# Sorted rows of the first halves loaded in blocks of 32 features and turned by VectorE

## Chip, cores and metric

The kernel runs on one core of a Trainium2 chip. The metric is the device time of one execution in microseconds; lower is better. The time before is the median of three runs.

## What is computed

The input x is (4, 32, 128, 128) in float32: four batches. Layer 0 splits each image into 128 channels of 64 x 64 positions and lets the channels' *columns* attend to each other within a batch. Layer 1 takes each batch as 8,192 rows of 128 features (written `t` below), adds linear attention, and then a mixture of experts:

```python
def _L1_ffn_ref(x, router_w, router_b, expert_w, expert_b):
    router_probs = jax.nn.softmax(x @ router_w + router_b, axis=-1)   # 8 experts
    top_p, top_i = jax.lax.top_k(router_probs, 2)
    top_p = top_p / jnp.sum(top_p, axis=-1, keepdims=True)
    expert_out = jnp.einsum('bnd,edc->bnec', x, expert_w) + expert_b
    gathered = jnp.take_along_axis(expert_out, top_i[..., None], axis=2)
    return jnp.einsum('bnk,bnkc->bnc', top_p, gathered)
...
t = t + _L1_attn_ref(_ln_t(t), L1_attn_Wk, L1_attn_Wq, L1_attn_Wv)
t = t + _L1_ffn_ref(_ln_t(t), L1_ffn_router_w, L1_ffn_router_b, L1_ffn_expert_w, L1_ffn_expert_b)
```

The change is in the experts: each row is multiplied by the 128 x 128 weights of its two experts only. The kernel handles a batch as 32 tiles of 128 rows, in two halves of 16 tiles.

## The kernel before

**The main loop: layer 0's attention, in ticks.** `attend` walks over blocks of 512 x 512 scores. One step of its inner loop is a *tick*: TensorE multiplies a 128 x 512 block of scores (L609, `pe<-qn,qn`), ScalarE takes its exponential (L612, `pr<-pe`), and two ticks later TensorE multiplies the result with the values (L497, `po<-pr,qT`). As scores are symmetric, each block is used a second time, turned: VectorE turns its 32 x 32 blocks (L421, `F<-pr`), `move` writes F to DRAM after four ticks (L530, `blocks<-F`, one DMA), and `bring`, three ticks later, reads it back with the groups of 32 swapped (L545, `F<-blocks`, six DMAs). The products with it (`transposed_share`, L433, `pg<-F,qT`) are put on a list (`late`) with a due time: LAG = 57 clock units after `bring`. A tick counts 8 units, and 4 more when it takes such a share, so with all three matmuls it counts 12. VectorE adds the result to the output (L442, `o<-o,pg`).

**The order.** Instructions of TensorE, VectorE, ScalarE and SP are kept in the order in which the program writes them. Other work is interleaved as generators: while batch b+1 runs through `attend`, the closing of batch b (`layer1`) is advanced by two yields a tick, one in front of the tick's matmuls and one behind them, at most once in PACE = 10 units. So one yield of `layer1` is half a tick.

**Layer 1 of a batch.** `close_rows` finishes layer 0's rows and normalises them; `attention_rows` adds the attention. Its input tiles are turned without TensorE already: `fetch_blocks` (L938, `blocks<-rows`) reads rows from DRAM in four DMAs, each bringing 32 features of all rows to 32 partitions, in pieces of 128 B, and VectorE turns the 32 x 32 blocks (L950). Then `route` chooses two experts for each row, and `sorted_experts(h)` runs for each half h. Batch 3 has no batch behind it to hide in: it multiplies all experts (`last_parts`) and doesn't sort. So `sorted_experts` runs for three first halves and three second halves.

**`sorted_experts(h)`.** It gives each (row, expert) pair of a half a place in a list sorted by expert, in which each expert's part begins at a new tile: NT = 2 x 16 + 8 - 1 = 39 tiles of 128 places. GpSimd scatters the rows with their weight to `xs[h]` in DRAM (L1066, rows of DW = 132 elements: 128 features, then the weight four times, 528 B). When all are there, the tiles are read, multiplied by the weights of the tile's expert, and written to `ys`; GpSimd then gathers two rows of `ys` for each token and adds them.

The read-and-multiply part is what changes. It takes the 39 tiles in 20 *pairs*. For each pair it

- loads both tiles with one DMA from SP (`load`, L1096, `xn<-xs`, 132 KB) into one of six buffers, which lie in the tile `xn` that the scattered rows came from,
- turns them on TensorE three steps later (L1137, `pys<-ident,xn`, 128 x 128 each) into a PSUM bank,
- copies the turned pair to SBUF with ScalarE (L1106, `xn<-pys`),
- multiplies each tile by its expert's weights (L1130, `pys<-ew_sb,xn`), at a column that TensorE reads from a register, in the step after,
- multiplies the result by the row's weight, which came in column D of the loaded tile, with VectorE (L1112, `results<-pys,xn`), and stores it (L1116, `ys<-results`, 128 KB).

A step is two yields, so one tick: the load, and the evictions of the step before, are at the first yield, the matmuls at the second. There are 25 steps, so 50 yields.

`hold` gives out the PSUM banks for such side work. At most three are held; when a fourth is asked for, the oldest is evicted at once. `wait_for` adds a wait: loads wait until all scatters of the half have landed, and the next batch's scatters wait for the loads.

Of the kernel before, what the change touches and what calls it, by code (L numbers as in the profile page):

```python
# [12 lines left out]
F32 = mybir.dt.float32  # L13
# [3 lines left out]
ALU = mybir.AluOpType  # L17
# [5 lines left out]
def kernel(  # L23
# [43 lines left out]
    nc = tc.nc  # L67
    P = 128
# [8 lines left out]
    S = 32  # L77
    NH, KQ, D = wk.shape
    E = router_w.shape[1]
# [10 lines left out]
    stat = ctx.enter_context(tc.tile_pool(name="stat", bufs=2))  # L90
# [27 lines left out]
    NT = 2 * HR + E - 1  # L118
    DW = D + 4
# [5 lines left out]
    ew_sb = const.tile([P, E, D], F32, tag="ew", name="ew_sb")  # L125
    xs = [dram.tile([NT * P, DW], F32, tag=f"xs{h}", name=f"xs_{h}", bufs=1) for h in range(2)]
    xs_made, xs_read = ([], []), ([], [])

    def wait_for(inst, others, why):
        for other in others:  # L130
            tc.add_manual_dep(
                inst, other.name, mybir.DependencyInfo(mybir.DependencyClass.Sync, mybir.DependencyReason.DATA),
                reason=why,
            )
# [56 lines left out]
    def hold(name, evict, alloc=psum_t):  # L191


        while len(held) >= banks[0]:
            held[0]()
        bank = alloc(name)

        def done():
            if done in held:
                held.remove(done)  # L200
                evict(bank)

        held.append(done)
        return bank, done
# [449 lines left out]
    def layer1(b, st):  # L654
# [3 lines left out]
        xn = big1.tile([P, KT, DW], F32, tag="xn", name=f"xn_{b}")  # L658
# [6 lines left out]
        begin = stat.tile([P, 2, NT + 1], U32, tag="begin", name=f"begin_{b}", bufs=1)  # L665
# [3 lines left out]
        keep = {}  # L669
# [273 lines left out]
        def attention_rows(u):  # L943
# [35 lines left out]
            if u % 2:  # L979
                for _ in route(u // 2):  # L980
                    yield
                    yield
                yield
                yield
                yield from sorted_experts(u // 2)

        def sorted_experts(h):
# [5 lines left out]
            half = slice(r0, r0 + HR)  # L993
# [21 lines left out]
            pc, done = hold(f"pcnt_{b}_{h}", lambda p: nc.vector.tensor_copy(counts.rearrange("p n e -> p (n e)"), p[:, : 2 * E]))  # L1015
# [5 lines left out]
            count = counts[:, 1, :][:, :, None]  # L1021
# [30 lines left out]
            ys = dram.tile([NT * P, D], F32, tag=f"ys{h}", name=f"ys_{b}_{h}")  # L1052

            def offset(ap):
                return bass.IndirectOffsetOnAxis(ap=ap, axis=0)
# [4 lines left out]
            for n in range(2 * HR):  # L1060
                i, k = n // HR, r0 + n % HR
                if n % HR == 0:
# [3 lines left out]
                inst = nc.gpsimd.indirect_dma_start(  # L1066
                    xs[h], offset(place[:, i, k : k + 1]), xn[:, k, :], None
                )
# [20 lines left out]
            bufs = [xn[:, r0 + 2 * i : r0 + 2 * i + 2, :] for i in range(8)]  # L1089
            pairs = [(g, min(2, NT - 2 * g)) for g in range((NT + 1) // 2)]  # L1090

            def rows_of(dram_rows, g, n):
                return dram_rows[2 * g * P : (2 * g + n) * P, :].rearrange("(j p) d -> p j d", p=P)

            def load(g, n):
                inst = nc.sync.dma_start(bufs[g % 6][:, :n], rows_of(xs[h], g, n))  # L1096
                wait_for(inst.ins, xs_made[h], "a tile holds tokens of any row")
                xs_read[h].append(inst.ins)

            def products(turned, applied):  # L1100


                def leave(p):
                    if turned:
                        g, n = turned
                        nc.scalar.activation(  # L1106
                            bufs[6 + g % 2][:, :n, :D], p[:, : n * P].rearrange("p (j t) -> p j t", t=P), AF.Copy
                        )
                    if applied:
                        g, n = applied  # L1110
                        result = keep["results"][:, g % 4]
                        nc.vector.tensor_tensor(  # L1112
                            result[:, :n], p[:, 2 * P : 2 * P + n * D].rearrange("p (j c) -> p j c", c=D),
                            bufs[g % 6][:, :n, D : D + 1].to_broadcast([P, n, D]), ALU.mult,
                        )
                        nc.sync.dma_start(rows_of(ys, g, n), result[:, :n])  # L1116

                p, done = hold(f"pys_{b}_{h}_{(turned or applied)[0]}", leave)
                if applied:
                    g, n = applied  # L1120
                    if g % 2 == 0:
                        _, at = nc.values_load_multi_w_load_instructions(
                            begin[0:1, h, 2 * g : min(2 * g + 4, NT)], engines=[mybir.EngineType.PE], min_val=0,
                            max_val=(E - 1) * D,
                            skip_runtime_bounds_check_because="D times a count of at most E - 1, never negative",
                        )
                        begins[:] = at
                    weights = ew_sb.rearrange("p e c -> p (e c)")
                    for j in range(n):
                        nc.tensor.matmul(  # L1130
                            p[:, 2 * P + j * D : 2 * P + j * D + D], bufs[6 + g % 2][:, j, :D],
                            weights[:, bass.ds(begins[2 * (g % 2) + j], D)], start=True, stop=True,
                        )
                if turned:
                    g, n = turned
                    for j in range(n):
                        nc.tensor.transpose(p[:, ts(j, P)], bufs[g % 6][:, j, :D], ident)  # L1137
                return done

            if "results" not in keep:  # L1140
                keep["results"] = work.tile([P, 4, 2, D], F32, tag="df", name=f"results_{b}", bufs=1)
            done = None
            begins = []
            for at in range(len(pairs) + 5):
                if at < len(pairs):
                    load(*pairs[at])
                if done:
                    done()
                yield
                turned, applied = (pairs[at - d] if 0 <= at - d < len(pairs) else None for d in (3, 4))  # L1150
                done = products(turned, applied) if turned or applied else None
                yield
            if done:
                done()
            if h == 1:
                st["sorted"] = True
            yield from idle(1)
# [271 lines left out]
    for b in range(B):  # L1429
# [12 lines left out]
        done = [0] * len(timed)  # L1442
        start = clock[0]
        closing = None
        for half, _ in enumerate(chain(attend(b, states[b]), finish() if b == B - 1 else ())):
            if half % 2 == 0:
                t = 100 * (clock[0] - start) / UNITS
# [64 lines left out]
```

## Time and profile before

| | us |
|---|---|
| median of 3 runs | 1651.85 (1651.45 to 1653.72) |
| the profiled execution | 1650.83 |
| its span, first to last instruction | 1649.0 |

The profile is of one execution. PE is TensorE's matmuls, PEld its weight loads, DVE is VectorE, ACT ScalarE, POOL GpSimd, SP the engine that issues most DMAs; "SPq" is its queue of instructions. Durations of matmuls overlap, since TensorE is pipelined, so the time that a matmul takes from the next is read in the chain of work that ended last rather than from its duration. A group's line gives the engine, the operation, what is written and read, the shape, the count, then busy us and mean ns, then idle time just before and what ended it. A line of waits gives total us, times, and the longest. A line of a stage window gives its length, then busy us and counts of PE, PEld, DVE, ACT and POOL, the granted clock, the mean busy share of the 16 DMA engines (it can exceed 1, as packets overlap) and GB/s.

The whole span by 40 slices of 41 us, the busy share in tenths: TensorE is at 8 or 9 in every slice but the last.

### The profile page before, as it was taken

How to read it: one execution, taken by the hardware profiler on the slowest of the kernel's cores; microseconds unless marked ns; L12 is line 12 of the kernel's file. 1: busy time of each engine (PE TensorE's matmuls, PEld its weight loads, DVE VectorE, ACT ScalarE, POOL GpSimd, SP SyncE). 2: the span in 40 equal slices, each digit the busy share in tenths (PEclk: the TensorE clock that was granted, in tenths of full speed). 3: DMA queues.
4: the chain of work that ended last, by engine and by line, in shares of the span. 5: the costliest groups of instructions: out<-in, count | busy, mean ns of one | idle time of the engine just before them, and what ended most of it. 6: DMA issues, size and time to landing. Idle time of an engine off the chain costs nothing.

```text
span 1649.0 us, 21309 instructions
## 1 busy us (share of the span) xinstructions
PE 1609.9 (98%) x5192; PEld 846.5 (51%) x5192; DVE 931.5 (56%) x2383; ACT 898.5 (54%) x2839; POOL 593.8 (36%) x565
## 2 busy tenths in 40 slices
PE   8999999999999999999999999999999999999987
PEld 4444544455554455555554455555554455555633
DVE  4543353567586443549478443448658634345786
ACT  3555445466475555547556455556656555545386
POOL 1000000001015441446555543256555652437166
PEclk9999999999999999999999999999999999999999
DMA  4655656676759777997899777798699877886001
GB/s 143 205 179 178 197 187 213 222 231 204 168 196 283 239 222 220 266 257 200 211 221 287 253 236 241 222 268 230 196 209 279 275 248 236 248 251 192 14 14 39
DMA packets 304297, 345.37 MB, mean 209 GB/s; under 512 B 82096, under 2 KB 230704, under 8 KB 289840
## 3 DMA queue, kind: packets, MB, share of 16 engines
q1 hardware_dynamic: 269712, 304.50, 59.9%
q0 software_dynamic: 26624, 25.58, 7.6%
q10 hardware_dynamic: 7840, 13.93, 2.9%
q8 instruction: 44, 0.72, 0.2%
q14 instruction: 77, 0.63, 0.1%
HBM read 167.08 MB, written 182.09 MB: 212 GB/s over the span
## 4 chain that ended last, share of the span: by engine, by line
PE 81%; DVE 7%; DMA 5%; ACT 3%; SPq 2%; issue 1%; POOL 1%; ACTq 0%; DVEq 0%; POOLq 0%
PE po L497 24%; PE pe L609 23%; PE pg L433 20%; PE pys L1130 3%; PE py L1304 3%; PE pg L453 2%; PE pys L1137 2%; PE pgram L725 2%; DMA F<-blocks 1%; DVE F L421 1%; DMA blocks<-rows 1%; SPq L938 1%; ACT pr L612 1%; ACT xn L696 1%; DMA blocks<-F 1%
## 5 line engine op out<-in xcount | busy, mean ns | idle before, releaser
L612 ACT ACTIVATE pr<-pe 128x512 f32<-128x512 f32 (+1 forms) x576 | 322.4, 560 | 547.5 <-PE pe L609 507.0
L497 PE MATMUL po<-pr,qT 128*128 128x512 f32 (+3 forms) x1152 | 549.4, 559 | 4.2 <-ACT o L502 3.9
L609 PE MATMUL pe<-qn,qn 128*128 128x512 f32 x896 | 458.8, 594 | 4.6 <-ACT pr L612 4.6
L433 PE MATMUL pg<-F,qT 128*128 128x512 f32 x880 | 449.8, 593 | 4.7 <-DMA F<-blocks 4.7
L421 DVE STREAM_TRANSPOSE F<-pr 128x512 f32<-128x512 f32 x440 | 305.4, 700 | 134.5 <-ACT pr L612 124.7
L497 PEld LDWEIGHTS po<-pr,qT 128*128 128x128 f32 x1152 | 215.2, 190 | 250.2 <-issue 217.9
L1178 POOL DMA_INDIRECT acc<-ys,place x128 | 202.1, 1579 | 209.1 <-ACT pr L612 134.8
L438 ACT ACTIVATE junk<-F 128x512 bf16<-128x512 f32 x440 | 273.0, 620 | 4.9 <-DMA F<-blocks 4.9
L433 PEld LDWEIGHTS pg<-F,qT 128*128 128x128 f32 x880 | 166.8, 190 | 199.4 <-issue 182.3
L1066 POOL DMA_INDIRECT xs<-xn,place x192 | 186.0, 969 | 184.1 <-ACT pr L612 118.9
L609 PEld LDWEIGHTS pe<-qn,qn 128*128 128x128 f32 x896 | 155.6, 191 | 119.1 <-issue 106.7
L442 DVE TENSOR_TENSOR o<-o,pg 128x512 f32<-128x512 f32 x110 | 75.1, 683 | 205.4 <-PE pg L433 205.2
L1112 DVE TENSOR_TENSOR results<-pys,xn 128x256 f32<-128x256 f32 x120 | 49.9, 416 | 187.2 <-ACT xn L1106 168.5
L164 POOL TENSOR_TENSOR rn<-ss,neg_half 128x8 f32<-128x8 f32 (+1 forms) x17 | 27.2, 1602 | 320.0 <-DVE ss L296 319.9
L612 ACT ACTIVATION_READ_ACCUMULATOR pr<-pe 128x1 f32 x576 | 111.9, 194 | 0.0
L1106 ACT ACTIVATE xn<-pys 128x256 f32<-128x256 f32 x120 | 45.2, 377 | 111.4 <-PE pys L1137 111.4
L1130 PEld LDWEIGHTS pys<-ew_sb,xn 128*128 128x128 f32 x468 | 70.5, 191 | 52.2 <-issue 49.7
L609 PE MATMUL pe<-qn 128*128 128x512 f32 (+3 forms) x256 | 91.4, 440 | 0.7 <-ACT qn L342 0.7
L1178 POOL DMA_INDIRECT yb<-ys,place x64 | 60.8, 950 | 81.1 <-DMA F<-blocks 31.1
L438 ACT ACTIVATION_READ_ACCUMULATOR junk<-F 128x1 f32 x440 | 84.5, 192 | 0.0
L1130 PE MATMUL pys<-ew_sb,xn 128*128 x468 | 71.6, 275 | 0.0
L1304 PE MATMUL py<-ew_sb,xn 128*128 128x512 f32 x128 | 61.5, 622 | 5.1 <-ACT tmp L1260 3.9
(217 smaller groups left out, 1463.2 us busy)
## 6 DMA issues: line engine op xcount, KB each, us to landing
blocks<-F SPq DMA_DIRECT2D x110, 1024.0 KB
F<-blocks SPq DMA_DIRECT2D x220, 192.0 KB
F<-blocks SPq DMA_DIRECT2D x220, 128.0 KB
xn<-xs SPq DMA_DIRECT2D x114, 132.0 KB
ys<-results SPq DMA_DIRECT2D x114, 128.0 KB
F<-blocks SPq DMA_DIRECT2D x220, 64.0 KB
below<-F SPq DMA_DIRECT2D x31, 384.0 KB
T<-in_x_dram SPq DMA_DIRECT2D x64, 128.0 KB
```

The costliest lines, as they stand in the source:

```text
L421: f()
L433: nc.tensor.matmul(pg.rearrange("p (a f) -> p a f", a=4), st["qT"][i][:, ib, :], G[:, :, ib], start=(ib == 0), stop=(ib == NJ - 1),)
L438: nc.scalar.activation(junk, G[:, :, ib], AF.Copy, accum_out=st["sums"][:, NJ * i + ib, jc : jc + 1])
L442: nc.vector.tensor_tensor(st["o"][jc], st["o"][jc], pg, ALU.add)
L497: nc.tensor.matmul(row["po"][:, lo:hi], qT[blk // NJ][:, blk % NJ, :], w, start=start, stop=(row["left"] == 0))
L609: nc.tensor.matmul(pe[:, c0:], qn[jc][:, ts(j, P)], qn[i][:, c0:], start=True, stop=True)
L612: nc.scalar.activation(pr[:, c0:], pe[:, c0:], AF.Exp, accum_out=sums[:, t, i : i + 1]).ins
L1066: inst = nc.gpsimd.indirect_dma_start(xs[h], offset(place[:, i, k : k + 1]), xn[:, k, :], None)
L1112: nc.vector.tensor_tensor(result[:, :n], p[:, 2 * P : 2 * P + n * D].rearrange("p (j c) -> p j c", c=D), bufs[g % 6][:, :n, D : D + 1].to_ ...
L1130: nc.tensor.matmul(p[:, 2 * P + j * D : 2 * P + j * D + D], bufs[6 + g % 2][:, j, :D], weights[:, bass.ds(begins[2 * (g % 2) + j], D)], st ...
L1178: inst = nc.gpsimd.indirect_dma_start(to, None, ys, offset(place[:, i, k : k + 1]), compute_op=op)
L1304: nc.tensor.matmul(bank, xn[:, k, :D], ew_sb[:, 4 * h : 4 * h + 4, :], start=True, stop=True)
```

## The change

For the first half (h = 0) of each sorting batch, the tiles are taken in ten *quads* of four tiles (the last has three). The second half keeps the steps above, now as the generator `turned_by_tensor`.

- `load_blocks` reads a quad's 512 rows with four DMAs from SP, 64 KB each. DMA q brings features 32q to 32q + 31 to partitions 32q to 32q + 31, row 32m + i to partition 32q + i, so that it moves pieces of 128 B (2,048 for a quad). The weights' columns are not read.
- `turn` turns all 32 x 32 blocks of the quad with one VectorE transpose, 128 x 512, into another buffer. That gives the four tiles with features on partitions.
- `four_products` reads four registers and makes four matmuls into one bank; its `leave`, one tick later, multiplies by the weights and stores the quad with one DMA of 256 KB.
- The weights of all 39 x 128 places are read once at the start of the half, into `factor`, by a DMA whose pieces are single elements: 4,992 of 4 B.
- Loads, and turned tiles, have two buffers each (`parts`), which lie in the half of `xn`.

In units of a yield, quad g is loaded at 4g, turned at 4g + 8, multiplied at 4g + 11 and evicted at 4g + 13; where a turn and a load fall together, the turn (of two quads before) comes first. The loop again has 4 x 10 + 10 = 50 yields.

```diff
+            room = xn[:, half, :].rearrange("p k w -> p (k w)")
+            parts = [room[:, 4 * DW * i : 4 * DW * i + 4 * D] for i in range(4)]
+            quads = [(g, min(4, NT - 4 * g)) for g in range((NT + 3) // 4)]
...
+            def load_blocks(g, n):
+                rows = xs[h][4 * g * P : (4 * g + n) * P, :D].rearrange("(m i) w -> i m w", i=S)
+                for q in range(4):
+                    read(
+                        nc.sync.dma_start(
+                            parts[g % 2][ts(q, S), : n * D].rearrange("i (m c) -> i m c", c=S), rows[:, :, ts(q, S)]
+                        )
+                    )
+
+            def turn(g, n):
+                nc.vector.transpose(parts[2 + g % 2][:, : n * D], parts[g % 2][:, : n * D])
+
+            def four_products(factor, g, n):
+
+                def leave(p):
+                    result = keep["results"].rearrange("p g j c -> p (g j) c")[:, ts(g % 2, 4)]
+                    nc.vector.tensor_tensor(
+                        result[:, :n], p[:, : n * D].rearrange("p (j c) -> p j c", c=D),
+                        factor[:, 4 * g : 4 * g + n].to_broadcast([P, n, D]), ALU.mult,
+                    )
+                    nc.sync.dma_start(
+                        ys[4 * g * P : (4 * g + n) * P, :].rearrange("(j p) d -> p j d", p=P), result[:, :n]
+                    )
+
+                p, done = hold(f"pys_{b}_{h}_{g}", leave)
...
+                for j in range(n):
+                    nc.tensor.matmul(
+                        p[:, ts(j, D)], parts[2 + g % 2][:, ts(j, D)],
+                        weights[:, bass.ds(begins[j], D)], start=True, stop=True,
+                    )
+                return done
+
+            def turned_by_vector():
+
+                factor = stat.tile([P, NT, 1], F32, tag="factor", name=f"factor_{b}_{h}", bufs=1)
+                read(nc.sync.dma_start(factor, xs[h].rearrange("(t p) w -> p t w", p=P)[:, :, D : D + 1]))
+                leaves = {}
+                for at in range(4 * len(quads) + 10):
+                    for first_at, act in (
+                        (8, turn), (0, load_blocks), (11, partial(four_products, factor)), (13, lambda g, n: leaves.pop(g)()),
+                    ):
+                        if at >= first_at and (at - first_at) % 4 == 0 and (at - first_at) // 4 < len(quads):
+                            g, n = quads[(at - first_at) // 4]
+                            made = act(g, n)
+                            if first_at == 11:
+                                leaves[g] = made
+                    yield
...
+            yield from (turned_by_tensor if h else turned_by_vector)()
```

More of the change, by code (lines that the diff above doesn't have):

```diff
@@ L1138, in products, with read @@
                 return done
+            room = xn[:, half, :].rearrange("p k w -> p (k w)")
+            parts = [room[:, 4 * DW * i : 4 * DW * i + 4 * D] for i in range(4)]
+            quads = [(g, min(4, NT - 4 * g)) for g in range((NT + 3) // 4)]
+            def read(inst):
+                wait_for(inst.ins, xs_made[h], "a tile holds tokens of any row")
+                xs_read[h].append(inst.ins)
+            def load_blocks(g, n):
[6 more added lines that the diff above has]
+                    )
@@ new lines, in turn @@
+            def turn(g, n):
[11 more added lines that the diff above has]
+                p, done = hold(f"pys_{b}_{h}_{g}", leave)
+                _, begins = nc.values_load_multi_w_load_instructions(
+                    begin[0:1, h, 4 * g : 4 * g + n], engines=[mybir.EngineType.PE], min_val=0,
+                    max_val=(E - 1) * D,
+                    skip_runtime_bounds_check_because="D times a count of at most E - 1, never negative",
+                )
+                weights = ew_sb.rearrange("p e c -> p (e c)")
+                for j in range(n):
+                    nc.tensor.matmul(
+                        p[:, ts(j, D)], parts[2 + g % 2][:, ts(j, D)],
+                        weights[:, bass.ds(begins[j], D)], start=True, stop=True,
+                    )
+                return done
@@ L1140, in sorted_experts, with turned_by_tensor @@
             if "results" not in keep:
                 keep["results"] = work.tile([P, 4, 2, D], F32, tag="df", name=f"results_{b}", bufs=1)
-            done = None
             begins = []
-            for at in range(len(pairs) + 5):
-                if at < len(pairs):
-                    load(*pairs[at])
+            def turned_by_tensor():
+                done = None
+                for at in range(len(pairs) + 5):
+                    if at < len(pairs):
+                        load(*pairs[at])
+                    if done:
+                        done()
+                    yield
+                    turned, applied = (pairs[at - d] if 0 <= at - d < len(pairs) else None for d in (3, 4))
+                    done = products(turned, applied) if turned or applied else None
+                    yield
@@ L1147, in sorted_experts @@
                 if done:
                     done()
[L1149 to L1154, printed above, removed]
+            yield from (turned_by_tensor if h else turned_by_vector)()
             if h == 1:
```

## The prediction

> **What bounds the kernel now.** I read the page's busy times first, then its chain of work that ended last, then the groups kept apart by shape, then the waits and the stage windows of the three first halves.
>
> ```profile
> PE 1609.9 (98%) x5192; PEld 846.5 (51%) x5192; DVE 931.5 (56%) x2383; ACT 898.5 (54%) x2839; POOL 593.8 (36%) x565
> ...
> PE 81%; DVE 7%; DMA 5%; ACT 3%; SPq 2%; issue 1%; POOL 1%; ACTq 0%; DVEq 0%; POOLq 0%
> ```
>
> TensorE is busy in 98% of the span and holds 81% of the chain; VectorE and ScalarE have almost half their time free. So an instruction that leaves TensorE inside a stage where TensorE never waits shortens the span by the time for which it delays the next matmul. Is TensorE without waits where the change acts? The first halves' product steps run from about 571 to 656 us (batch 0), 964 to 1050 (batch 1) and 1328 to 1403 (batch 2); the second halves follow. The windows (span; busy us of PE, PEld, DVE, ACT, POOL; clock; DMA share; GB/s), three with first halves and two with second halves:
>
> ```profile
> 571.00:656.00 85.00, 84.64 (x296) 45.84 (x295) 36.16 (x69) 44.27 (x139) 28.81 (x30) 1.00 0.74 228
> 964.00:1050.00 86.00, 85.82 (x299) 46.48 (x298) 33.86 (x65) 44.44 (x139) 26.40 (x28) 1.00 0.71 223
> 1340.00:1425.00 85.00, 85.00 (x318) 47.99 (x317) 31.61 (x63) 45.07 (x140) 28.04 (x31) 1.00 0.75 230
> 660.00:740.00 80.00, 80.00 (x290) 44.22 (x289) 39.33 (x81) 40.64 (x127) 39.02 (x25) 1.00 0.97 265
> 1055.00:1135.00 80.00, 79.50 (x286) 43.93 (x285) 44.16 (x92) 41.62 (x130) 38.86 (x26) 1.00 0.97 265
> ```
>
> TensorE is full in all of them at full clock. The DMA engines are at 0.71 to 0.75 in the first halves, and at 0.97 in the second halves, where TensorE still loses at most 0.5 us of 80. The waits of TensorE on data through DRAM are small over the whole span:
>
> ```profile
> PE pg L433 <- DMA F<-blocks: 4.7, 3, 1.9
> ```
>
> **What the Trainium skill says.** "TensorE: Matmul & The Clock Gate", Part 4 (PE-mode transpose), gives about 275 ns for a transpose in a kernel; the trace has 273 ns as its duration, but durations overlap on TensorE, so I don't price with it. "VectorE: DVE Perf Modes", The three transpose paths, says that VectorE turns 32x32 blocks only, so the blocks must be placed by the load; the trace already has this pair of steps in the attention rows (L938, L950). The DMA prices come from "DMA: Bandwidth & Descriptors" and are used below.
>
> **The change, part by part.**
>
> ```profile
> L1137 PE MATMUL pys<-ident,xn 128*128 128x128 f32 x234 | 45.2, 273 | 0.7 <-DMA xn<-xs 0.7
> L1106 ACT ACTIVATE xn<-pys 128x256 f32<-128x256 f32 x114 | 43.6, 382 | 108.5 <-PE pys L1137 108.5
> L1112 DVE TENSOR_TENSOR results<-pys,xn 128x256 f32<-128x256 f32 x114 | 48.2, 423 | 180.9 <-ACT xn L1106 168.5 <-issue 5.2 <-DMA F<-blocks 3.8
> L950 DVE STREAM_TRANSPOSE xnT<-blocks 128x512 f32<-128x512 f32 x24 | 16.4, 692 | 23.9 <-PE pat L855 14.2 <-DMA blocks<-rows 9.7
> ```
>
> (1) *Transposes removed.* Each first half has 39 tiles, so 117 of the 234 transposes of L1137 go (batch 3 doesn't sort). In the chain of the window 571 to 656, L1137 has 5.0% of 85 us = 4.25 us; in 964 to 1050, 5.0% of 86 = 4.3 us. That is 0.109 us for a transpose, and the chain's pieces agree: 0.22 us for each pair between product and score matmul. Three halves: 4.25 + 4.3 + 39 x 0.109 = **12.8 us off the path**. The products (L1130) stay, four in a burst each second tick instead of two each tick, at 0.22 us each in the chain either way; the register loads stay one for four tiles.
>
> (2) *ScalarE.* 20 evictions of L1106 for each half leave, 20 x 0.38 = 7.6 us. ScalarE is busy 44 of 85 us and TensorE doesn't wait for it: nothing.
>
> (3) *VectorE.* Added for each half: 10 turns at 0.69 us (row L950, same shape). The multiplications become 10 of 128x512 at about 0.69 us (a 128x512 add from PSUM, L442, is 683 ns) for 20 of 0.42 us. So +6.9 + 6.9 - 8.4 = +5.4 us, to some 42 of 81 us. Off the path, as VectorE is half idle. A turn is a new kind of wait in VectorE's order, though: it waits for a load, and the transposes into F, the additions into o and the multiplications stand behind it.
>
> (4) *DMA work.* Removed: 2.6 MB for each half in 528 B rows; at the 393 to 418 GB/s that windows with larger rows show when the engines are full, 6.6 us of all 16 engines. Added: 39 x 128 x 4 = 19,968 rows of 128 B. The trace has such rows in L938, nearly alone here (four DMAs of 1,024 rows, issued from 429.2):
>
> ```profile
> 431.00:432.00 1.00, 1.00 (x4) 0.43 (x3) 0.85 (x2) 0.30 (x2) 0.00 (x0) 1.00 1.06 166
> 432.00:433.00 1.00, 1.00 (x4) 0.52 (x3) 0.00 (x0) 0.42 (x1) 0.00 (x0) 1.00 1.10 169
> 433.00:434.00 1.00, 1.00 (x3) 0.38 (x3) 0.70 (x1) 0.88 (x4) 0.00 (x0) 1.00 0.95 125
> ```
>
> The 0.52 MB pass in about 3.65 us: 4,096 rows x 14 ns / 16. So 19,968 x 14 / 16 = 17.5 us. L938's rows lie 512 B apart, the new ones 528 B apart and so mostly off 256 B boundaries; the skill's DMA page, How a descriptor splits into AXI transactions, charges beats from the boundary below: by its rule I count 8 beats of 32 B on average where L938's rows need 6. Adding three beats of fixed cost (same page, Why small descriptors are slow), my estimate is 14 x 11/9 = 17 ns, or 21 us, as the upper end; no run here shows it. I take 17.5, so +10.9 us. The *factor* load adds 4,992 pieces of 4 B. No row here shows such a piece. Lower bound: the same page's 10.5 ns a packet (Measured): 4,992 x 10.5 / 16 = 3.3 us. Upper: VectorE's page calls a strided plain copy 19 times slower than 1.309 us for 128x128, 24.9 us for 16,384 elements, so 7.6 us for 4,992. I take 5. The sum: 0.74 x 85 = 63 us now, +10.9 + 5 = 79 of 81 us, a share of 0.97: what the second halves have now with TensorE full. That is the cover. Each F has room: L545 is issued at 601.8, landed by about 608, and the shares are due LAG 57 after, 57/12 ticks or some 14 us after, so about 7 us later than it lands.
>
> (5) *SP's queue.* For four ticks (about 12 us): before, 4 loads x 0.42 + 4 stores x 0.39 + 7 DMAs of F (2.7 + 0.37) = 6.3 us. After: 8 loads at about 0.55 (between 0.42 and L938's 0.56 to 0.74) + 2 stores x 0.4 + 3.1 = 8.3 us. +2 us in 12, or 13 to 14 us for a half; SP waits there 29.3 us for results alone:
>
> ```profile
> SPq L1116 <- DVE results L1112: 29.3, 11, 9.1
> ```
>
> A load also waits for the turn of two quads before, queued in the same step; the wait replaces part of that idle time. Behind it stand the stores and F's six reads, with the 7 us of room. The stores themselves become half as many.
>
> (6) *Order and start.* A half keeps 50 yields (25 ticks), so nothing later moves by ticks. A quad's load has four ticks (12 us) to its turn and 5.5 to its products (16.6 us). Loads now land in 2.3 to 5.9 us, median 4.1; with 2.2 us of issue, 1.8 of transfer and a wait for F's reads ahead of it I expect 8 to 10. Tightest is the first quad: no products run yet, so 4 ticks are 10.3 us and 5.5 are 14.2; ahead of it go the factor's issue (some 0.4 to 1.4 us) and its 3.3 to 7.6 us. That sums to 11 to 15 us: VectorE waits up to 4 us there, and TensorE 0 to 1.5 us. I take 0.6 us a half, **+1.9 us**.
>
> **Sum.** -12.8 + 1.9 = -10.9 us. The profiled execution took 1650.83 us with a span of 1649.0, so its span would be about 1638; against the median, 1.0 us above the profiled run, 1651.85 - 10.9 = **1641.0 us**. All hidden: 1639.
>
> **Rivals.**
> *The cover is partly gone* (0.17): late loads and late F reads cost TensorE 2 to 4 us in each half, 6 to 11 us in all, eating most of the gain: 1645 to 1650, centre 1647. For: the stretch 820 to 860, where L938's 128 B rows meet gathers, has a DMA share above 1 and TensorE loses about 1.8 us at 840 to 860. Against: at 0.97 it loses none in 660 to 740.
> *DMA becomes the bound of the first halves* (0.11; slower): if a 128 B row off its boundary costs 28 ns, twice L938's, and the factor 7.6 us, the work is 63 - 6.6 + 35 + 7.6 = 99 us in 81. Less the 7 us of room, TensorE stalls 11 us a half, 33 in all: 1652 - 12.8 + 33, about 1672. It begins to stall at about 21 ns a row and turns the sign when a half loses over 4.3 us, at about 25 ns.
> *The gain isn't there* (0.04): the transposes go, but the burst of four products opens a gap of equal size on TensorE, since they wait for the turn 1.5 ticks before: about 1652.
>
> **How the numbers follow.** My forecast (1639 to 1644) has 0.68. About 0.2% (3.3 us) is what a measurement here can tell from no change. Faster by more: 0.68 + 0.13 of the partial case = 0.81; within: 0.04 + 0.04 + 0.01 = 0.09; slower by more: 0.10. The range goes from 1638 (12.8 us and a little from freed banks) through the partial case to 1651; outside stay the slow case and half of the no-gain case.
>
> **What would show it.** Right: no L1137 transposes in the first halves, TensorE full there, each of these stages shorter by about 4 us, DMA share near 0.95, turns at about 0.7 us, F's waits on TensorE under 3 us more in total. Step 4 is wrong if a quad's load lands later than about 12 us after issue; step 6 is wrong if the first product of a half waits for its turn by over 2 us; step 1 is wrong if the stages shorten by less with no new wait.

## The result and the profile after

| | before, us | after, us |
|---|---|---|
| median of 5 runs | 1651.45 (1649.40 to 1653.72) | 1635.17 (1633.65 to 1638.94) |
| the profiled execution | 1650.83 | 1638.94 |
| its span | 1649.0 | 1637.1 |

The ratio is 0.9904, 95% interval 0.9891 to 0.9917: 16 us faster, where 10.9 us were forecast. The profiled execution of the changed kernel is the slowest of its five, so the two profiles differ by less, 11.9 us. That difference between profiled and timed executions comes up again below.

The page of the changed kernel: busy time, DMA packets, chain of work.

```profile
PE 1598.4 (98%) x5075; PEld 832.8 (51%) x5075; DVE 942.7 (58%) x2383; ACT 877.2 (54%) x2779; POOL 593.8 (36%) x565
...
DMA packets 364728, 345.18 MB, mean 211 GB/s; under 512 B 157504, under 2 KB 291136, under 8 KB 350272
...
PE 84%; DVE 6%; DMA 4%; ACT 2%; issue 1%; POOL 1%; SPq 1%; ACTq 0%; DVEq 0%; POOLq 0%
```

TensorE has 117 matmul instructions fewer (5192 before) and still fills 98% of the span. The DMA engines move as many bytes in 60,000 packets more. TensorE's share of the chain is 84% for 81% before. Repeats of the changed kernel, below, have 81 to 84%, so this difference says nothing; TensorE is the bound in both kernels.

The groups kept apart by shape show the new steps (count, busy us, mean ns, then the idle time before and what ended it):

```profile
L1180 PE MATMUL pys<-ew_sb,xn 128*128 x234 | 31.0, 275 | 0.0
L1137 PE MATMUL pys<-ident,xn 128*128 128x128 f32 x117 | 22.6, 273 | 0.0
L1164 DVE TENSOR_TENSOR results<-pys,factor 128x512 f32<-128x512 f32 x27 | 18.4, 682 | 3.4 <-PE pys L1180 3.4
L1158 DVE STREAM_TRANSPOSE xn<-xn 128x512 f32<-128x512 f32 x27 | 18.2, 675 | 0.1
```

L1180 has the products of the quads, a pair of instructions for each of the 117 tiles, and TensorE was never idle before one. Half of L1137's transposes are left, the second halves'. The turns of L1158 find their loads landed: 0.1 us of idle time in front of 27 of them.

The stage windows, three in first halves and one in a second half (columns as before):

```profile
573.00:656.00 83.00, 82.82 (x263) 42.83 (x262) 40.44 (x70) 37.94 (x122) 28.80 (x30) 1.00 0.88 235
964.00:1047.00 83.00, 82.82 (x264) 42.83 (x264) 38.42 (x66) 37.92 (x120) 26.95 (x29) 1.00 0.84 235
1323.00:1398.00 75.00, 75.00 (x244) 39.46 (x243) 33.37 (x56) 34.21 (x109) 26.97 (x29) 1.00 0.96 258
656.00:736.00 80.00, 80.00 (x288) 43.87 (x287) 39.24 (x80) 40.77 (x126) 39.02 (x25) 1.00 0.97 261
```

TensorE is full in all four. The prediction's third window before, 1340 to 1425, reached into batch 2's second half, whose transposes begin at 1406. A window of the first half alone, of the kernel before, shows much the same:

```profile
1322.00:1402.00 80.00, 80.00 (x279) 43.42 (x278) 29.03 (x55) 42.36 (x133) 31.73 (x35) 1.00 0.76 238
```

So the DMA share of the first halves went from 0.71 to 0.76 up to 0.84 to 0.96, and TensorE still did not wait: the cover held.

Windows that end at fixed times hold different work in two kernels. A cleaner measure is the time from the start of one po product (L497) to that of a later one, both counted in TensorE's order, which neither kernel changes:

| po products, stage | before, us | after, us | transposes put back, us |
|---|---|---|---|
| 456 to 528, batch 0, first half | 104.86 | 100.60 | 104.88 |
| 744 to 816, batch 1, first half | 104.86 | 100.60 | 104.88 |
| 1008 to 1068, batch 2, first half | 85.76 | 81.50 | 85.78 |
| 1068 to 1104, batch 2, second half | 54.47 | 53.58 | 53.58 |
| 528 to 672, batch 0, second half and on | 196.63 | 198.86 | 196.66 |

The last column is the second run of an experiment below. Each first half is shorter by 4.26 us, and every repeat of the changed kernel shows 100.60 in batches 0 and 1, to the hundredth. In batch 2 the two repeats on chips without the pauses described below show 81.50; the two on chips with them show 84.04 and 85.53, for 89.57 before. The fourth row gives 0.89 us more. Before, the one wait of L1137 on a load (the 0.7 us in its row in the prediction) lay at 1459.9, near the end of that second half's transposes (1406 to 1469):

```profile
1460.58 0.44 PE L1137 MATMUL pys<-ident,xn 128*128 128x128 f32 x2 [0.67 <-DMA xn<-xs]
```

It is absent in this profile and in the two repeats on chips without pauses, but a repeat on a chip with pauses has 1.5 us of it at the same place, so the change does not remove it for good. The fifth row goes the other way. Two of four repeats have 196.31 and 196.70 there, and a kernel in which batch 0 is left as before (only_batch_2, below) has 198.64, so it is not from the change in batch 0.

### The profile page after: what moved, and what is told of

Read it like the earlier page. It is cut to its first block, busy times and chain, and to the rows that moved or that the text cites. A ratio compares the mean times of both kernels' runs of the same rounds, so it can differ in the third digit from the quotient of the medians.

```text
span 1637.1 us, 20938 instructions
## 1 busy us (share of the span) xinstructions
PE 1598.4 (98%) x5075; PEld 832.8 (51%) x5075; DVE 942.7 (58%) x2383; ACT 877.2 (54%) x2779; POOL 593.8 (36%) x565
## 4 chain that ended last, share of the span: by engine, by line
PE 84%; DVE 6%; DMA 4%; ACT 2%; issue 1%; POOL 1%; SPq 1%; ACTq 0%; DVEq 0%; POOLq 0%
PE po L497 25%; PE pe L609 24%; PE pg L433 21%; PE py L1371 3%; PE pg L453 2%; DMA F<-blocks 2%; PE pys L1180 2%; PE pys L1130 2%; PE pgram L725 2%; PE pat L855 1%; SPq L545 1%; DMA below<-F 1%; PE pys L1137 1%; ACT xn L696 1%; ACT pr L612 1%
## 5 line engine op out<-in xcount | busy, mean ns | idle before, releaser
L497 PE MATMUL po<-pr,qT 128*128 128x512 f32 (+3 forms) x1152 | 549.8, 559 | 4.2 <-ACT o L502 3.5
L497 PEld LDWEIGHTS po<-pr,qT 128*128 128x128 f32 x1152 | 215.6, 191 | 251.5 <-issue 219.4
L1112 DVE TENSOR_TENSOR results<-pys,xn 128x256 f32<-128x256 f32 (+1 forms) x60 | 24.9, 416 | 83.5 <-ACT xn L1106 70.4
L164 POOL TENSOR_TENSOR rsa<-dm_a,neg_half 128x8 f32<-128x8 f32 x16 | 28.9, 1807 | 104.7 <-DVE sv_a L688 104.6
L696 ACT ACTIVATE xn<-T,nbo,rsf 128x128 f32<-128x128 f32 x128 | 54.1, 495 | 20.7 <-POOL nbo L692 20.7
L164 POOL TENSOR_TENSOR rsf<-dm_f,neg_half 128x8 f32<-128x8 f32 (+1 forms) x15 | 26.3, 1751 | 105.2 <-DVE sv_f L688 105.2
```

The costliest lines, as they stand in the source:

```text
L164: pinned(nc.gpsimd.tensor_tensor(dst, src, neg_half.to_broadcast(list(src.shape)), ALU.pow))
L497: nc.tensor.matmul(row["po"][:, lo:hi], qT[blk // NJ][:, blk % NJ, :], w, start=start, stop=(row["left"] == 0))
L696: nc.scalar.activation(xn[:, k, :D], T[:, k, :], AF.Identity, scale=rs[:, k, :], bias=nb[:, k, :])
```

## The experiments

Theory A: the gain is what the transposes took on TensorE's path, 12.8 us, and the rest is scatter, for instance in how often TensorE ran at half clock. Theory B: other parts of the change, such as taking the tiles by fours, give about 3 us by themselves. All comparisons are with the kernel before on the same chip. On two of the chips (those where the kernel before stands at 1662 us) both kernels took some 10 us more than on the others.

**The changed kernel again**, on four occasions, and the kernel before with a second profile.

> The changed kernel once more, for its median beside the kernel before on the same chip and for the granted clock of each execution. Theory A (the 117 transposes off TensorE's path are the whole gain, 12.8 us; what the first comparison showed beyond that, 3.5 us, comes from how many stretches of half clock TensorE had in an execution): 12 to 14 us faster than the kernel before once executions of equal mean clock are compared. Theory B (other parts of the change, ScalarE's relief or fewer stores, bring a further 3 us): 15 to 17 us faster at equal clock too.

> The changed kernel a third time, beside the one that leaves the turning out. Theory A (the gain is the 12.8 us of transposes; the 3.5 us beyond it are chance, stalls and half-clock stretches of TensorE that fall differently): over three comparisons the mean gain comes down toward 13 to 14 us, and this kernel is within 2 us of no_turn_again. Theory B (the grouping itself brings 3 us): 16 us again, 3 to 5 us faster than no_turn_again.

> The changed kernel, fourth comparison, on one chip with the next two. Three comparisons give 16.0 us of gain (plus or minus 1.6, weighted), where the trace shows 12.8 in the first halves. Theory A (nothing but the transposes): 12.8 us faster than the kernel before, give or take 3. Theory B (the rest of the change brings about 3 us elsewhere): 16 us.

> The kernel before, for a second profile of it: its own stalls and half-clock stretches. Theory A: the stages with first halves' products take 104.9 us again, and the differences to the first profile lie elsewhere, in stretches at half clock. Theory B expects nothing of this run.

| changed kernel | us | before, us | ratio (95%) |
|---|---|---|---|
| after_again | 1646.28 | 1662.15 | 0.9900 (0.9885 to 0.9916) |
| after_third | 1648.09 | 1661.93 | 0.9911 (0.9879 to 0.9943) |
| after_fourth | 1636.79 | 1652.00 | 0.9900 (0.9885 to 0.9915) |
| after_fifth (with the last group) | 1636.29 | 1653.34 | 0.9894 (0.9877 to 0.9910) |

With the result itself these are five comparisons. Weighted by their intervals they give 0.9901 +- 0.0007, or 16.4 +- 1.2 us. The differences of the medians alone are 16.3, 15.9, 13.8, 15.2 and 17.0 us. So the excess over 12.8 us is no accident of the first measurement.

Nor is it the clock. The record has the mean granted clock of each timed execution, so executions of equal clock can be compared, as after_again's expectation asks. With after_fourth the changed kernel is 16.4, 17.7 and 15.4 us faster at 0.995, 0.996 and 0.997; with after_fifth 16.7, 17.4 and 18.5 us at 0.996, 0.997 and 0.998 (one to six executions on each side). On the chips with pauses it is 12.3 to 16.8 us. Theory A expected 12 to 14.

The second profile of before took 1663.46 us. Its waits, above, beside those of the first profile of before, below:

```profile
ACT pr L612 <- issue: 36.2, 45, 1.5
```

```profile
ACT pr L612 <- issue: 2.6, 2, 1.5
```

"Issue" is time in which an engine waited for nothing that the trace shows. On this chip ScalarE has 36 us of it. Apart from 2.8 us in the first 100, these pauses begin at about 510 us, and the late stages are longer (po products 1008 to 1068: 89.57 us for 85.76; 1104 to 1128: 48.00 for 42.47). The changed kernel has such pauses on these chips too (49 and 47 us of them in after_again and after_third), so both sides of a ratio have them; what makes them stays open.

**The transposes put back**, ahead of the product, which overwrites what they write. Loads, turns, quads and ScalarE's share stay as in the changed kernel. Run twice.

```diff
                 for j in range(n):
+                    nc.tensor.transpose(p[:, ts(j, D)], parts[2 + g % 2][:, ts(j, D)], ident)
+                for j in range(n):
                     nc.tensor.matmul(
```

> The changed kernel, with one TensorE transpose put back for each tile of the first halves, ahead of its product and overwritten by it; no ScalarE copy. Theory A: 12.8 us slower than the changed kernel, level with the kernel before within 2 us. Theory B: 3 us of the gain stay, so 10 us slower than the changed kernel or less, and 3 us faster than the kernel before.

> The changed kernel with the first halves' TensorE transposes put back, again: all of the change but the time on TensorE. It was 1.3 us faster than the kernel before (plus or minus 1.6). Theory A: within 1.5 us of the kernel before. Theory B: 3 us faster than the kernel before.

Measured: 1660.95 us, ratio 0.9992 (0.9982 to 1.0002), and 1652.12 us, ratio 0.9997 (0.9988 to 1.0005); together -0.8 +- 1.1 us. The chain of the window 573 to 656 by line, of the changed kernel:

```profile
by line: PE po L497 30.9%; PE pe L609 28.5%; PE pg L433 27.4%; PE pys L1180 10.5%; PE pg L453 1.6%; ACT o L502 0.6%; ACT pr L612 0.5%; PE pnorm L399 0.5%; issue 0.4%
```

and with the transposes put back, where L1180 is the transpose and L1182 the product:

```profile
by line: PE po L497 28.8%; PE pe L609 26.9%; PE pg L433 25.9%; PE pys L1182 10.5%; PE pys L1180 5.1%; PE pg L453 1.6%; ACT o L502 0.6%; ACT pr L612 0.5%; PE pnorm L399 0.5%; issue 0.4%
```

The transposes take their 5.1% of 83 us = 4.2 us again, and the stage is back at 104.88 us. The rest of the change, with the transposes in place, is worth 0.8 +- 1.1 us, which agrees with the 0.9 us of batch 2's second half in the table above. So Theory B's source falls (3 us from the quads and the rest by themselves), though its number fits the repeats.

**The transposes left out of the kernel before**, first halves only, with ScalarE's copies; the products take the unturned rows, so the first halves' expert products are of other data. Nothing of the loads or of VectorE changes. Run three times.

```diff
-                    if turned:
+                    if turned and h == 1:
...
-                            p[:, 2 * P + j * D : 2 * P + j * D + D], bufs[6 + g % 2][:, j, :D],
+                            p[:, 2 * P + j * D : 2 * P + j * D + D],
+                            (bufs[6 + g % 2] if h == 1 else bufs[g % 6])[:, j, :D],
...
-                if turned:
+                if turned and h == 1:
...
-                done = products(turned, applied) if turned or applied else None
+                done = products(turned, applied) if (turned and h == 1) or applied else None
```

> The kernel before with the first halves' transposes and ScalarE copies left out and the loads, multiplications and stores as before: the products take the rows unturned. Theory A: as fast as the changed kernel within 2 us, 12.8 us faster than the kernel before; the block loads, the factor load and the turns of the changed kernel then cost nothing. If they do cost something that is hidden in the sum, this kernel is faster than the changed one by that. Theory B with the stores as its source: slower than the changed kernel by 3 us.

> The kernel before without the first halves' transposes and ScalarE copies (the products take unturned rows), again. Theory A: 12.8 us faster than the kernel before, within 2 us of the changed kernel. Theory B: 10 to 11 us faster than the kernel before as in the first comparison, and 3 to 5 us slower than the changed kernel.

> The kernel before without the first halves' transposes and ScalarE copies, with the old loads and stores (the products take unturned rows), again: the TensorE part alone. It was 10.7 and 14.1 us faster than the kernel before. Theory A: 12.8 us faster and level with the changed kernel. Theory B: 12.8 us faster and 3 us behind the changed kernel.

Measured: 1651.54, 1647.29 and 1638.06 us, ratios 0.9935 (0.9922 to 0.9949), 0.9915 (0.9887 to 0.9942) and 0.9916 (0.9903 to 0.9930); together -12.5 +- 1.5 us. The first halves take 100.60 us, as in the changed kernel, and 54.33 follows instead of 53.58: the wait of batch 2 stays. The removal alone gives what the first step said. The changed kernel reaches the same stage time, so all that it adds is hidden there. Against the changed kernel on the same chip this kernel is 5.3 us slower, 0.8 us faster and 1.3 us slower: the first run fits Theory B, the other two Theory A. The removal alone and the rest alone (transposes_back) add up to 13.3 +- 1.9 us, of the 16.4 +- 1.2.

**Both halves turned by VectorE.**

```diff
-                factor = stat.tile([P, NT, 1], F32, tag="factor", name=f"factor_{b}_{h}", bufs=1)
+                factor = stat.tile([P, NT, 1], F32, tag=f"factor{h}", name=f"factor_{b}_{h}", bufs=1)
...
-            yield from (turned_by_tensor if h else turned_by_vector)()
+            yield from turned_by_vector()
```

> The changed kernel with the second halves done in the same way as the first (each half with its own factor tile). Theory A: another 117 transposes leave TensorE, 12.8 us more gain, if the DMA engines still follow; the second halves have a DMA share of 0.97 already, and 11 us of work more in some 76 us of stage would take it to about 1.1. Rival (the DMA engines become the bound there): 78 + 11 = 89 us of work in 76 us, less 7 us of room, so some 6 us of stall a half, 18 in all, and the kernel is 5 us slower than the changed one.

Measured: 1674.61 us, ratio 1.0081 (1.0062 to 1.0100), 28 us above the changed kernel on the same chip; the rival had expected about 5. Two second halves in windows, and then the waits of this kernel:

```profile
656.00:740.00 84.00, 80.56 (x264) 41.95 (x263) 45.29 (x83) 36.86 (x118) 42.13 (x27) 1.00 1.02 256
1055.00:1140.00 85.00, 79.62 (x255) 41.07 (x254) 48.89 (x97) 35.61 (x114) 37.46 (x25) 0.98 0.99 250
```

```profile
DVE xn L1158 <- DMA xn<-xs: 56.3, 19, 6.0
...
PE po L497 <- ACT o L502: 13.6, 15, 10.0
DVE results L1164 <- DMA ys<-results: 13.1, 9, 2.4
PE pg L433 <- DMA F<-blocks: 11.2, 7, 2.7
```

These two second halves stood at a DMA share of 0.97 before; with the same small rows added they stand at about 1, and TensorE loses 3 to 5 us in each window. The turn now waits 56 us for its loads, in VectorE's order, and the stores and F's reads come late behind it. This fits the rival "DMA becomes the bound", in the half that the change leaves alone: 0.74 had room for it and 0.97 had not. It is not shown alone: in the first of these windows DMAs have some 16% of the chain (F's reads 7.5%), but SP's issues of loads and F's reads have 10%, and no run separates the two.

The 28 us are not even. By po products, and against after_again, the stretches with the second halves of batches 0, 1 and 2 are 6, 8 and 15 us longer. Batch 2's has the longest wait of the second line, 10.0 us from 1435 on, and from 1440 on the clock is halved for 10.2 us. VectorE and ScalarE waited there too, for something that the trace doesn't name, and the chip is one with pauses. The kernel's executions have a mean clock of 0.988, for 0.994 or 0.995 of the changed kernel beside it, so a part of the 28 us is half clock behind such waits.

**The factor load four times**, three of them into unused room of the results, all ahead of the first quad's load: 10 us more work of the DMA engines (an estimate: 14,976 packets of 4 B at 10.7 ns, over 16 engines) at the most sensitive place.

```diff
+                spare = keep["results"].rearrange("p g j c -> p (g j c)")[:, 4 * D :]
+                for i in range(3):
+                    read(
+                        nc.sync.dma_start(
+                            spare[:, ts(i, D)][:, :NT, None], xs[h].rearrange("(t p) w -> p t w", p=P)[:, :, D : D + 1]
+                        )
+                    )
```

> The changed kernel with the factor load issued four times, three of them into unused room, all ahead of the first quad's load: 10 us more of DMA work at each start, in 14,976 pieces of 4 B. If the start of a half has the room that the trace of the changed kernel shows (first turn without a wait, products 5 us after it), TensorE waits 3 to 6 us in each half and the kernel is 10 to 17 us slower than the changed one. If the start was as tight as the prediction had it, 25 to 30 us slower. If the cover is wider, under 3 us slower.

Measured: 1654.39 us, ratio 0.9948 (0.9934 to 0.9962), 6.3 us above the changed kernel on the same chip, between the expectation's wider cover (under 3) and its first case (10 to 17). Its waits:

```profile
DVE xn L1158 <- DMA xn<-xs: 60.8, 27, 7.6
...
PE pys L1180 <- DVE xn L1158: 5.0, 3, 2.5
```

Three times, once in each half, TensorE waits for a turn, up to 2.5 us; the first halves of batches 0 and 1 take 101.60 and 103.32 us for 100.60. The delay comes by SP's queue: the three added issues hold SP for 9.6 us, and in batches 0 and 1 the first quad lands 16.4 us after the factor's issue instead of 7.9. So with 8.5 us more the start is too late by 0.7 to 2.5 us, and the single factor load leaves some 6 to 8 us of room. The trace of the changed kernel agrees: the first quads' loads land 2.8 to 3.9 us before their turns, and the turns end 3.0 to 5.2 us before the products.

**One part of the batches.** The timed gain is larger than the sum of what the traces place. Is the remainder one batch's? Batch 2 alone, and batches 0 and 1 alone, with the changed kernel beside them:

```diff
-            yield from (turned_by_tensor if h else turned_by_vector)()
+            yield from (turned_by_tensor if h or b < 2 else turned_by_vector)()
```

and with `b == 2` for `b < 2`. A and B in these expectations are theories on the remainder.

> The changed kernel again, beside the two kernels that change one part of the halves. Both theories: about -16 us against the kernel before (0.990), of which 12.8 us are the transposes that left TensorE's path and 0.9 us a wait that is gone in the second half of batch 2. Theory A (the remainder of 2 to 3 us is spread over the executions, not tied to one batch): single batches give their share. Theory B (it belongs to one batch): one of the two kernels beside it has it whole.

> Only batch 2's first half is turned by VectorE; batches 0 and 1 keep the transposes. The trace should show 104.86 us in the first halves of batches 0 and 1 and 81.50 in batch 2's, with 53.58 instead of 54.47 at the start of its second half on a chip without pauses. Theory A (a remainder that isn't tied to one batch): 4.26 + 0.89 + a third of the remainder, -5 to -6.5 us. Theory B (the remainder belongs to batch 2): -7.5 to -9 us, and the kernel with batches 0 and 1 alone gives no more than 8.5.

> Only the first halves of batches 0 and 1 are turned by VectorE; batch 2 keeps the transposes. The trace should show 100.60 us in both and 85.75 in batch 2's. Theory A: 2 x 4.26 + two thirds of the remainder, -9 to -10.5 us. Theory B (the remainder belongs to batch 2): -8.5 us and no more. If it belongs to batches 0 and 1 instead: -11 us or more, and batch 2 alone gives about -5.

| kernel | us | ratio (95%) | gain, us | placed by the stages, us |
|---|---|---|---|---|
| only_batch_2 | 1645.75 | 0.9958 (0.9944 to 0.9972) | 6.9 +- 2.3 | 4.4 |
| only_batches_0_1 | 1640.18 | 0.9919 (0.9906 to 0.9933) | 13.4 +- 2.2 | 8.0 |
| after_fifth | 1636.29 | 0.9894 (0.9877 to 0.9910) | 17.5 +- 2.7 | 13.7 |

The stages are as expected to 0.02 us (104.86 or 100.60 in batches 0 and 1, 85.75 or 81.50 in batch 2), with one miss: batch 2 alone has 54.33 in the row in which I expected 53.58. Its wait at the end of the second half is there, 0.5 us, and with batches 0 and 1 alone it is 1.2 us and the row 54.98, which is why 8.0 us are placed and not 8.5. Each kernel gains 2.5 to 5.4 us more than its stages show. Batches 0 and 1 gain 13.4 +- 2.2 without batch 2, where "the remainder belongs to batch 2" allowed 8.5 and no more, so that is refuted. Theory A missed as well: both gains lie above its ranges, the second beyond its interval. The third case, that the remainder belongs to batches 0 and 1, had expected 11 us or more and about 5; it is not excluded. The gains of the two parts add up to 20.3 us, +- 3.2 or more, as both are measured against the same executions of before. So a remainder spread evenly fits no better than a constant one.

## Why the prediction was partly wrong

The mechanism was right: the transposes left TensorE's path and the rest of the change stayed hidden. The forecast of 1641.0 us was 5.8 us above the measured time, which lies below the range. Of these 5.8 us, 1.9 are step 6, which failed, 0.4 are that before had a median of 1651.45 us in this comparison and not 1651.85, and 3.5 are gain beyond step 1, for which the sum had no term and the range left 1 us.

*Step 1, transposes removed: right.* 12.8 us were priced from the chain. The stages give 4.26 + 4.26 + 4.26 = 12.8 us, the removal alone 12.5 +- 1.5 us, and putting them back takes it away. The row's 273 ns would have given 117 x 0.273 = 32 us.

*Steps 2 and 3, ScalarE and VectorE: right.* A turn takes 675 ns and a multiplication 682 (0.69 each forecast). VectorE is busy 40 of 83 us, and ScalarE 38.

*Step 4, DMA work: right in what it decides, wrong in two prices.* A 128 B packet takes 13.8 to 14.0 ns on average in the three halves, the value taken. The 17 ns that I counted by the beats of the Trainium skill, "DMA: Bandwidth & Descriptors", How a descriptor splits into AXI transactions, are not seen. The factor's packets take 10.7 ns, 4,992 x 10.7 / 16 = 3.3 us, the lower bound. That bound met it by luck: the 10.5 ns of the Trainium skill, "DMA: Bandwidth & Descriptors", Measured, are one transfer's 0.67 us divided by its 64 packets, and the prediction divided by 16 engines once more. The profile of before could have given the price, as its 32,689 packets of 4 B took 10.8 ns on average. The removed 528 B rows took 32 ns each in the profile of before, 4,992 x 32 / 16 = 10 us a half and not 6.6. So the net is 17.5 + 3.3 - 10 = +10.8 us and not +15.9, and the windows agree: 0.88 x 83 - 0.74 x 85 = +10.1 us. That is why the share is 0.88 and 0.84 where I expected 0.97; batch 2's first half, in a shorter window of 75 us, has 0.96.

*Step 5, SP's queue: right.* SP's waits in 573 to 652 on results, 29.3 us before:

```profile
SPq L1168 <- DVE results L1164: 6.0, 3, 3.0
```

The wait shrinks by more than the 13 to 14 us of added issue, and nothing behind it is late. TensorE's wait on F, 4.7 us before:

```profile
PE pg L433 <- DMA F<-blocks: 4.6, 3, 2.3
```

*Step 6, order and start: this failed.* I added 1.9 us since the first quad would land 11 to 15 us after the start, with 10.3 us to its turn and 14.2 to its products. (The parts as I listed them, 0.4 to 1.4, 3.3 to 7.6 and 8 to 10 us, add up to 11.7 to 19.) SP's queue at the start of batch 0's half (start, us, instruction):

```profile
573.00 0.39 SPq L1189 DMA_DIRECT2D factor<-xs  x1
573.49 5.63 SPq L1152 DMA_DIRECT2D xn<-xs  x4
579.24 2.80 SPq L545 DMA_DIRECT2D F<-below  x6
582.08 2.07 SPq L1152 DMA_DIRECT2D xn<-xs  x4
```

The four issues take 5.63 us (the first of them 4.02), two and a half times what I had put down. Even so the last packet has landed 7.5 us after the first of them (7.4 and 7.1 in the other batches), or 7.5 to 8.0 us after the factor's issue. In batch 0 the factor's packets move from 1.5 to 5.1 us after that issue, while SP is held by the first load, and the quad's from 5.1 to 7.9 us, while SP issues the other three. So transfers run under issues, where I had added them one after the other. Over all quads the median from first issue to landing is 5.3 us, where I expected 8 to 10. The added wait is 0, and the sum becomes 1651.85 - 12.8 = 1639.0, my "all hidden".

*The range* ended only 1 us below that, and the measured 1635.2 is 3.9 us further, so mending step 6 alone would not have been enough. Of the excess of 16.4 +- 1.2 over 12.8, 0.9 us is batch 2's second half, where the wait of L1137 at 1459.9 is absent. Its row showed it, and I gave it no price. 2.7 +- 1.2 us remain that no stage carries, and their cause stays open. It isn't the work by fours (transposes_back: -0.8 +- 1.1), nor the removal (12.5 +- 1.5), each by itself, and not batch 2 alone.

Single executions do differ by such amounts. The same stretch of the changed kernel in two executions, its first profile and then after_fifth's:

```profile
848.40:851.80 3.40, 3.40 (x5) 1.39 (x5) 0.00 (x0) 2.16 (x7) 0.09 (x1) 0.51 0.98 310
```

```profile
848.40:851.80 3.40, 3.40 (x12) 1.82 (x11) 1.40 (x3) 3.37 (x11) 1.57 (x1) 1.00 0.68 164
```

In the first TensorE ran at half clock, just after an idle gap of 2.3 us, and made 5 matmuls instead of 12; in the second the gap was 1.86 us, and no such stretch came. Gap and stretch together are the 198.86 us of the table's fifth row; after_fifth has 196.70. The first 24 po products differ in the same way, 21.06 us against 19.15. The one profile of before on these chips is free of both. But such stretches do not carry the remainder. At equal clock the gain is as large, as shown above, and the timed executions of before have a mean clock of 0.9962 and 0.9963 on the two chips without pauses where the record lists them, while its profile has 0.996. The timed median of before lies 0.6 to 2.5 us above that profile (1651.45 to 1653.34 against 1650.83). And outside the four stages that the change shortens, the eight profiles on chips without pauses take 1297.8 to 1300.9 us, in no order by kernel: 1299.1 before, 1297.8 to 1300.9 in the changed kernel. So no profile shows where the remainder lies.

*The rivals.* The partly gone cover and the gain that isn't there are refuted by full windows and by first halves of 100.60, 100.60 and 81.50 us. The DMA bound did not come in the first halves, at 14 ns a row where it needed 21 to begin; what both_halves shows in the second halves fits it.

## What to carry to other kernels

Price an instruction that leaves a busy TensorE by its share in the chain of its stage, not by its duration (0.109 us against 0.273 here). Before work is moved from TensorE to finer loads and an idle VectorE, read the DMA share of that very stage: the same step cost nothing at 0.74, and 6 and 8 us net at 0.97 (second halves of batches 0 and 1). Put a price, or a place in the range, on each wait that the row of a removed instruction shows. Compare timed executions of equal granted clock before a remainder is put down to the clock.

## What was not expected of the hardware

- TensorE ran at half clock for stretches of 3.4 us (now and then 6.8 or 10.2), at places that differ between executions of one kernel; a stretch of 3.4 us costs up to 1.7 us. In the middle of the span (60 to 1500 us) of all the traces, none came after the ten idle gaps of 1.72 to 1.87 us, and some after gaps of 1.92 us and more, though not after each (none after one of 2.95 us).
- On two of the chips ScalarE and VectorE pause, from about 510 us on, for nothing that the trace shows: 36 us on ScalarE for 2.6 (before), and some 10 us of time for both kernels.
- A packet of 528 B took 32 ns, of 128 B 14.0, and of 4 B 10.7, and rows of 128 B that lie 528 B apart were no dearer than the attention rows 512 B apart, from which the price was taken.
- The issue of a block load on SP, 0.50 us in the median, took 3.3 to 4.4 us for the first load of each half, directly behind the factor's 4,992 pieces of 4 B, in all five profiles of the changed kernel. In factor_x4 each issue directly behind a factor load took 2.7 to 3.8 us.
